# Soft mixture of experts inside a three-stage model: where the first weight transposes, the experts' loops and the combine weights' softmax stand

## Chip, cores and metric

The kernel runs on one core of a Trainium2 chip, in one launch. The metric is the time on the device in microseconds (us), the median of several runs. The inputs are drawn from a fixed seed, and all arithmetic is in float32.

## What is computed

Two blocks with a residual each, over x of shape (2, 1024, 256):

```python
x = x + L0_ffn(L0_cond(x, cond), phi, W, b)     # attention with 16 heads, then the soft mixture
x = x + L1_ffn(L1_cond(x, cond), ...)           # a rotation, then two layers of windowed attention
```

The change lies in the soft mixture, `L0_ffn`, with 64 experts of 32 slots each (2048 slots):

```python
logits   = einsum("bmd,dnp->bmnp", x, phi)
dispatch = softmax(logits, axis=0)                          # over the two batches
combine  = softmax(logits.reshape(b, m, n * p), axis=-1)    # over all 2048 slots
slots    = einsum("bmd,bmnp->bnpd", x, dispatch)
y        = einsum("bnpd,nde->bnpe", slots, W) + b[None, :, None, :]
out      = einsum("bnpd,bmnp->bmd", y, combine)
```

## The kernel before

The order of work on TensorE (PE), VectorE (DVE) and ScalarE (ACT) is written out by hand: inside a `manual_schedule` block each of these engines takes its instructions in the order in which the Python code issues them, and waits in that order. SyncE (SP) issues nearly all DMAs, also in one order. A tile pool hands out its buffers in turn, and a new tile waits until the last reader of the buffer's previous holder is done.

**First half of the mixture.** A loop over `it` from 0 to 31 takes a block of 512 slots (`n`) and a block of 128 tokens of each batch (`m`). `logits(it)` (L795) makes the logits of both batches in PSUM, copies them into a tile `keep` (ACT L803, DVE L806), issues two stores of 256 KB from `keep` to a scratch tensor `lgd` (L808), and takes the softmax over two batches as two sigmoids (L810, L811). `keep` has a ring of two buffers. `dispatch(it)` (L821) adds into the slots; at `m == 7` the sums are copied to the tile `slots`, batch 0 by ACT (L830) and batch 1 by DVE (L831). `experts(g0)` multiplies two groups of four experts by their weights (L842), 32 matmuls into one PSUM tile `py`, and adds the bias (DVE L851); it then issues the loads of the next two groups, 1 MB each (L778).

**Second half.** `ebig` holds four rows of 128 tokens by 2048 slots, row i in place i % 4. For each row, `fetch` (L864) brings the logits back from `lgd` in four pieces, `heaviest(i)` finds the maximum (DVE L868, L869), `weigh(i)` takes the exponential and its sum (ACT L875) and `scale(i)` divides (DVE L880, L881). `turn_w(q, jj)` transposes one of four pieces of rows 2q and 2q + 1 (PE L888, eight transposes into PSUM), copies it to a place in `xb` (ACT L895 for odd `jj`, DVE L897 for even `jj`), and issues the fetches of the same piece of rows 2q + 4 and 2q + 5. `combine(q, jj)` multiplies it by y (PE L909, eight matmuls); after `jj == 3` the result is added to x (DVE L920). The copies of `turn_w` cannot use `xb` before the last `dispatch`, since `xo_tm`, the tokens that `dispatch` reads, lies in the same memory.

PSUM tiles of `logits`, `turn_w`, `experts` and `rotate` all come from one ring of two buffers, `wide`. The loop around the change runs `q` from 0 to 3 and, within it, `jj` from 0 to 3: each round issues `turn_w` of the next piece, then `combine` of this one, then steps of the softmax of later rows; `rotate(0)` (L929, four matmuls of 512 columns) comes in round `q == 2`. Rounds 4 to 7 are interleaved with the next stage.

Of the kernel before, what the change touches and what calls it, by code (L numbers as in the profile page):

```python
# [10 lines left out]
F32 = mybir.dt.float32  # L11
# [6 lines left out]
P = 128  # L18
B = 2
S = 1024  # L20
# [71 lines left out]
def tile_kernel(ctx: ExitStack, tc: tile.TileContext, a: dict, out: bass.AP):  # L92
# [23 lines left out]
    xb = res.tile([P, 2, B, S + 1], F32, name="xb")  # L116
# [597 lines left out]
    for u in range(len(units)):  # L714
        if u % 2 == 0 and u + 2 < len(units):
            b, g = units[u + 2]
# [29 lines left out]
    with tc.manual_schedule(  # L746
        engines={mybir.EngineType.PE, mybir.EngineType.DVE, mybir.EngineType.Activation}
    ):
        for s in range(STEPS):
            u, p = s // 16, s % 16 // 2  # L750
# [38 lines left out]
    def logits(it):  # L789

        n, m = divmod(it, 8)
        lg = wide("lg")
        for b in (1, 0):
            for k in range(2):
                nc.tensor.matmul(  # L795
                    lg[:, b, :],
                    xa[:, k, b, 1 + m * P : 1 + (m + 1) * P],
                    phi[:, k, n * 512 : (n + 1) * 512],
                    start=(k == 0),
                    stop=(k == 1),  # L800
                )
        keep = dx0.tile([P, B, 512], F32, tag="keep", name="keep")
        nc.scalar.copy(keep[:, 1, :], lg[:, 1, :])  # L803
        l1 = dx0.tile([P, 512], F32, tag="l1", name="l1")
        nc.vector.tensor_tensor(l1, lg[:, 0, :], keep[:, 1, :], ALU.subtract)  # L805
        nc.vector.tensor_copy(keep[:, 0, :], lg[:, 0, :])  # L806
        for b in range(B):
            nc.sync.dma_start(lgd[b * 8 + m][:, n * 512 : (n + 1) * 512], keep[:, b, :])  # L808
        dsps[it] = dx0.tile([P, B, 512], F32, tag="dsp", name="dsp")
        nc.scalar.activation(dsps[it][:, 0, :], l1, AF.Sigmoid)  # L810
        nc.scalar.activation(dsps[it][:, 1, :], l1, AF.Sigmoid, scale=-1.0)  # L811

    def dispatch(it):

        n, m = divmod(it, 8)
        if m == 0:
            accs[n] = [pair(f"sl{b}") for b in range(B)]
        d = dsps.pop(it)
        for b in range(B):
            for c in range(2):  # L820
                nc.tensor.matmul(  # L821
                    accs[n][b][:, c, :],
                    xo_tm[:, b * 8 + m, c * P : (c + 1) * P],
                    d[:, b, :],
                    start=(m == 0),
                    stop=(m == 7),
                )
        if m == 7:
            slots[n] = dx.tile([P, 2, B, 512], F32, tag="slots", name="slots", bufs=1)
            nc.scalar.copy(slots[n][:, :, 0, :], accs[n][0])  # L830
            nc.vector.tensor_copy(slots[n][:, :, 1, :], accs[n][1])  # L831

    def experts(g0):

        py = wide("py").rearrange("p x (b d) -> p x b d", b=B)
        for x in range(2):
            w = ws.pop(g0 + x)
            for b in range(B):
                for k in range(2):
                    for n in range(4):  # L840
                        s0 = (4 * ((g0 + x) % 4) + n) * NP
                        nc.tensor.matmul(  # L842
                            py[n * NP : (n + 1) * NP, x, b, :],
                            slots[g0 // 4][:, k, b, s0 : s0 + NP],
                            w[:, n, k, :],
                            start=(k == 0),
                            stop=(k == 1),
                        )
        i = g0 % 4
        for b in range(B):  # L850
            nc.vector.tensor_tensor(y[b][:, g0 : g0 + 2, :], py[:, :, b, :], ybs[g0 // 4][:, i : i + 2, :], ALU.add)  # L851
        for g in (g0 + 2, g0 + 3):
            if g < NE // 4:
                weights(g)
# [11 lines left out]
    def heaviest(i):  # L866
        nmxs[i] = wsm.tile([P, 1], F32, tag="nmx", name="nmx")
        nc.vector.tensor_reduce(nmxs[i], row(i), AX.X, ALU.max)  # L868
        nc.vector.tensor_scalar(nmxs[i], nmxs[i], -1.0, None, ALU.mult)  # L869
# [8 lines left out]
    def scale(i):  # L878
        den = dens.pop(i)
        nc.vector.reciprocal(den, den)  # L880
        nc.vector.tensor_scalar(row(i), row(i), den, None, ALU.mult)  # L881

    def turn_w(q, jj):

        pt = wide("pe")
        for j in range(4):
            for i in range(2):
                nc.tensor.transpose(  # L888
                    pt[:, j // 2, (j % 2 * 2 + i) * P : (j % 2 * 2 + i + 1) * P],
                    row(2 * q + i)[:, (4 * jj + j) * P : (4 * jj + j + 1) * P],  # L890
                    ident,
                )
        wTs[q, jj] = xb[:, jj % 2, 1, 1 : 1 + S].rearrange("p (x n) -> p x n", x=2)
        if jj % 2:
            nc.scalar.copy(wTs[q, jj], pt)  # L895
        else:
            nc.vector.tensor_copy(wTs[q, jj], pt)  # L897
        for i in (2 * q + 4, 2 * q + 5):
            if i < T // P:
                fetch(i, jj)  # L900
# [68 lines left out]
    with tc.manual_schedule(  # L969
        engines={mybir.EngineType.PE, mybir.EngineType.DVE, mybir.EngineType.Activation}  # L970
    ):
        at_weigh = (1, 3, 4, 6)
        for g in range(2):
            weights(g)
        for it in range(3, ITS):
            n, m = divmod(it, 8)
            if it + 1 < ITS:
                logits(it + 1)
            dispatch(it)
            if n and m in (1, 4):  # L980
                experts(4 * n - 4 + m // 4 * 2)

            i = it - ITS + 8
            if 0 <= i < 4:
                for jj in range(4):
                    fetch(i, jj)
            if i - 1 in at_weigh:
                scale(at_weigh.index(i - 1))
            if i in at_weigh:
                heaviest(at_weigh.index(i))  # L990
                weigh(at_weigh.index(i))
        turn_w(0, 0)
        turn_w(0, 1)
        experts(12)
        combine(0, 0)
        turn_w(0, 2)
        combine(0, 1)
        turn_w(0, 3)
        combine(0, 2)
        experts(14)  # L1000
        dxs.close()
        for t in (xa, xb):
            nc.gpsimd.memset(t[:, :, :, 0:1], 0.0)


        load = {}
        wqo = pphi.tile([P, 4 * D * 4], F32, tag="phi", name="wqo")
        load["wqkv"] = wqo[:, : 6 * INNER].rearrange("p (k n) -> p k n", k=2)
        load["wo"] = wqo[:, 6 * INNER :].rearrange("p (k n) -> p k n", k=4)
        mask = dx0.tile([P, 4 * WIN], F32, tag="l1", name="mask")  # L1010
        nc.sync.dma_start(mask, a["mask"])

        def weights2(l, *names):
            for name in names:
                if name == "tabs":

                    load[name] = [dx0.tile([P, 2, 8, DH], F32, tag="dsp", name=f"tabs{l}{y}") for y in range(2)]
                    for y, t in enumerate(load[name]):
                        nc.sync.dma_start(t, a["tabs"].rearrange("p (x y) w d -> y p x w d", y=2)[y])
                        for x, of in enumerate((("qs", "ks"), ("qsr", "ksr"))[y]):  # L1020
                            nc.gpsimd.tensor_tensor(
                                t[:, x], t[:, x], bcast(rows[:, ROWS[f"{of}{l}"]], 1, 8), ALU.mult
                            )
                    continue
                k = {"wqkv": 2, "wo": 4, "w1": 2, "w2": NF}[name]
                whole = HID // P if name == "w2" else k
                nc.sync.dma_start(
                    load[name][:, :whole, :], a[name][l, : whole * P].rearrange("(c p) n -> p c n", p=P)
                )
                if whole < k:  # L1030
                    for r0 in (0, TG):
                        nc.sync.dma_start(load[name][r0 : r0 + TAIL, whole, :], a[name][l, whole * P :])

        weights2(0, "wqkv", "tabs", "wo")
    with tc.manual_schedule(
        engines={mybir.EngineType.PE, mybir.EngineType.DVE, mybir.EngineType.Activation}
    ):
        for q in range(4):
            for jj in range(4):
                if q == 0 and jj < 3:  # L1040
                    continue
                turn_w(*divmod(4 * q + jj + 1, 4))
                combine(q, jj)

                i = 2 * q + 2 + jj
                if q and 1 <= jj < 3:
                    scale(i - 1)
                if q and jj < 2:
                    heaviest(i)
                    weigh(i)  # L1050
                if q == 2 and jj == 1:
                    rotate(0)
# [619 lines left out]
```

## Time and profile before

Times are from one profiled execution, in us from its start.

| | |
|---|---|
| median of 3 runs | 1625.15 us (1624.53 to 1625.74) |
| the profiled execution | 1625.17 us, of which the span from first to last instruction is 1623.2 |
| granted TensorE clock | 0.999 |
| PE busy 750 to 800 / 800 to 885 us | 48.90 of 50 / 83.09 of 85 |
| DVE busy, the same | 23.59 / 48.13 |
| ACT busy, the same | 16.14 / 30.03 |
| DMA engines' busy share, the same | 0.71 / 0.33 |

A row of the timeline gives start, duration, engine, line, operation, output tile <- inputs, tile shape, and in brackets the idle time of that engine just before it with what ended it. One fp32 matmul appears as two records, a transpose as one. A row of the waits gives who waited, for whom, the total in us, how often, and the longest.

The first half of the mixture ends at 763 us and the rounds `q` 0 to 3 end at 848 us.

### The profile page before, as it was taken

How to read it: one execution, taken by the hardware profiler on the slowest of the kernel's cores; microseconds unless marked ns; L12 is line 12 of the kernel's file. 1: busy time of each engine (PE TensorE's matmuls, PEld its weight loads, DVE VectorE, ACT ScalarE, POOL GpSimd, SP SyncE). 2: the span in 40 equal slices, each digit the busy share in tenths (PEclk: the TensorE clock that was granted, in tenths of full speed). 3: DMA queues.
4: the chain of work that ended last, by engine and by line, in shares of the span. 5: the costliest groups of instructions: out<-in, count | busy, mean ns of one | idle time of the engine just before them, and what ended most of it. 6: DMA issues, size and time to landing. Idle time of an engine off the chain costs nothing.

```text
span 1623.2 us, 22628 instructions
## 1 busy us (share of the span) xinstructions
PE 1591.8 (98%) x8660; PEld 803.4 (49%) x8660; DVE 941.9 (58%) x1605; ACT 884.8 (55%) x1653; POOL 538.3 (33%) x830
## 2 busy tenths in 40 slices
PE   8999999999999999999999999999999999999998
PEld 4333333333333444444877676555555555655543
DVE  4768758776763122225446755757576666666632
ACT  2477767777886222235234544656657575656531
POOL 3233323333330100000103434555565555465411
PEclk9999999999999999999999999999999999999999
DMA  5100000010000544546532002000100001000001
GB/s 157 52 14 14 1 16 12 1 21 8 1 1 27 169 141 151 178 148 195 184 126 78 27 1 80 1 1 1 65 1 0 14 1 54 1 6 22 14 14 39
DMA packets 49707, 82.65 MB, mean 51 GB/s; under 512 B 4536, under 2 KB 24928, under 8 KB 49344
## 3 DMA queue, kind: packets, MB, share of 16 engines
q1 hardware_dynamic: 47056, 75.38, 15.0%
q0 software_dynamic: 1584, 5.29, 1.1%
q8 instruction: 68, 1.11, 0.3%
q10 hardware_dynamic: 960, 0.56, 0.1%
q14 instruction: 39, 0.32, 0.1%
HBM read 56.04 MB, written 20.97 MB: 47 GB/s over the span
## 4 chain that ended last, share of the span: by engine, by line
PE 89%; DVE 6%; ACT 2%; POOL 1%; issue 1%; DMA 1%; DVEq 0%; ACTq 0%; POOLq 0%
PE pga L1371 8%; PE sc L329 8%; PE po L347 7%; PE pm L295 7%; PE lg L795 7%; PE sl L821 7%; PE pq L1121 6%; PE cmb L909 5%; PE pwo L1310 3%; PE po L1290 3%; PE sc L1210 3%; PE py L1396 3%; PE pv L1177 3%; PE pe L1271 3%; PE pqk L265 2%; PE py L842 2%
## 5 line engine op out<-in xcount | busy, mean ns | idle before, releaser
L302 DVE TENSOR_REDUCE mx<-pm 128x2 f32<-128x1024 f32 x256 | 302.5, 1220 | 117.9 <-PE pm L295 117.3
L337 ACT ACTIVATE e<-sc 128x512 f32<-128x512 f32 (+1 forms) x500 | 266.2, 611 | 72.2 <-PE pm L295 44.6
L329 PE MATMUL sc<-qs,km 32*128 32x512 f32 x1024 | 254.7, 619 | 0.9 <-DVE qs L317 0.9
L295 PE MATMUL pm<-km,qm 32*128 32x512 f32 x1024 | 246.0, 619 | 2.4 <-ACT xa L432 0.6
L365 POOL TENSOR_TENSOR ob<-ob,part 128x512 f32<-128x512 f32 x101 | 128.4, 1271 | 270.2 <-ACT part L364 270.2
L1227 DVE CUSTOM_DVE_ANT_0 e<-sc,mask,zn 128x256 f32<-128x256 f32 (+1 forms) x256 | 102.3, 463 | 69.5 <-PE sc L1210 69.5
L1371 PE MATMUL pga<-hc,w 128*128 128x512 f32 x320 | 141.1, 593 | 0.0
L1260 POOL TENSOR_SCALAR e<-e,den 128x256 f32<-128x256 f32 (+1 forms) x128 | 131.1, 1038 | 27.0 <-DVE den L1256 27.0
L347 PE MATMUL po<-e,v 128*32 128x512 f32 x1024 | 136.7, 604 | 0.0
L329 PEld LDWEIGHTS sc<-qs,km 32*128 32x128 f32 x1024 | 87.5, 183 | 84.6 <-ACT e L337 64.4
L1244 ACT ACTIVATE e<-e,nmx 128x256 f32<-128x256 f32 (+1 forms) x256 | 123.5, 485 | 1.9 <-DVE nmx L1227 1.6
L1145 POOL TENSOR_TENSOR t<-raw,tabs 128x512 f32<-128x512 f32 x64 | 81.5, 1295 | 124.8 <-ACT raw L1135 119.6
L1121 PE MATMUL pq<-wqo,xa 128*128 128x512 f32 x256 | 115.9, 595 | 1.6 <-DVE xb L897 0.9
L909 PE MATMUL cmb<-xb,y 128*128 128x256 f32 x512 | 116.6, 380 | 0.2 <-ACT xb L895 0.2
L795 PE MATMUL lg<-phi,xa 128*128 128x512 f32 x256 | 115.9, 595 | 0.3 <-ACT xa L432 0.3
L821 PE MATMUL sl<-dsp,xb 128*128 128x512 f32 x256 | 114.9, 592 | 0.0
L295 PEld LDWEIGHTS pm<-km,qm 32*128 32x128 f32 x1024 | 82.8, 183 | 60.0 <-DVE mx L302 31.7
L805 DVE TENSOR_TENSOR l<-lg,keep 128x512 f32<-128x512 f32 x32 | 22.1, 692 | 143.5 <-ACT keep L803 143.5
L909 PEld LDWEIGHTS cmb<-xb,y 128*128 128x128 f32 x512 | 94.9, 190 | 16.6 <-issue 3.2
L1135 ACT COPY raw<-pq 128x1024 f32<-128x1024 f32 x32 | 32.4, 1013 | 128.6 <-PE pq L1121 126.8
L1371 PEld LDWEIGHTS pga<-hc,w 128*128 128x128 f32 x320 | 59.2, 190 | 67.2 <-issue 63.9
L803 ACT COPY keep<-lg 128x512 f32<-128x512 f32 x32 | 18.7, 585 | 125.1 <-issue 107.4
(212 smaller groups left out, 2491.2 us busy)
## 6 DMA issues: line engine op xcount, KB each, us to landing
lgd<-keep SPq DMA_DIRECT2D x64, 256.0 KB, 2.4
w<-in_ffn_W SPq DMA_DIRECT2D x16, 1024.0 KB, 7.5
ebig<-lgd SPq DMA_DIRECT2D x64, 256.0 KB, 3.3
wqo<-in_wqkv SPq DMA_DIRECT2D x2, 1536.0 KB, 8.6
w<-in_w SPq DMA_DIRECT2D x2, 1386.0 KB, 5.9
km<-hk SPq DMA_DIRECT2D x32, 64.0 KB, 2.3
qm<-hq SPq DMA_DIRECT2D x32, 64.0 KB, 2.3
phi<-in_phi SPq DMA_DIRECT2D x1, 2048.0 KB, 7.6
```

What stands on the lines that cost most here:

```text
L295: nc.tensor.matmul(pm[:, x, :], qm[u % 2][r, i * P : (i + 1) * P], km[u % 3][r, n * 512 : (n + 1) * 512], start=True, stop=True,)
L302: nc.vector.tensor_reduce(mxs[hu][:, i % 4, 2 * half : 2 * half + 2, n], pm, AX.X, ALU.max)
L329: nc.tensor.matmul(sc[:, x, :] if both else sc[x], km[u % 3][r, j * P : (j + 1) * P], qs[u % 2][r, n * 512 : (n + 1) * 512], start=True, s ...
L337: nc.scalar.activation(part, t, AF.Exp, scale=1.0 / HD0**0.5)
L347: nc.tensor.matmul(po[32 * hh : 32 * hh + 32, :], v[b][:, j, at : at + 32], es[s, hh // 2][:, hh % 2, :], start=True, stop=True,)
L365: nc.gpsimd.tensor_tensor(obs[u, n], obs[u, n], part, ALU.add)
L795: nc.tensor.matmul(lg[:, b, :], xa[:, k, b, 1 + m * P : 1 + (m + 1) * P], phi[:, k, n * 512 : (n + 1) * 512], start=(k == 0), stop=(k == 1),)
L821: nc.tensor.matmul(accs[n][b][:, c, :], xo_tm[:, b * 8 + m, c * P : (c + 1) * P], d[:, b, :], start=(m == 0), stop=(m == 7),)
L909: nc.tensor.matmul(acs[q][:, c, :], y[b][:, 4 * jj + j, c * P : (c + 1) * P], eT[:, j // 2, j % 2 * 256 : (j % 2 + 1) * 256], start=(jj == ...
L1121: nc.tensor.matmul(pq[:, x, :], shifted(xa, k, b, w * WIN, P), load["wqkv"][:, k, x * 512 : (x + 1) * 512], start=(k == 0), stop=(k == 1),)
L1260: engine.tensor_scalar(e[:, x, c, lo:], e[:, x, c, lo:], den[:, x, c : c + 1], None, ALU.mult)
L1371: nc.tensor.matmul(pt[:, x, :], load["w1"][:, k, lo : lo + P], hcs[f][:, k, :], start=(k == 0), stop=(k == 1))
```

## The change

It has three parts. `experts` goes batch by batch over both weight groups instead of group by group over both batches. `turn_w(0, 0)` is issued before the last `dispatch`, and its copy goes to a tile of its own, `wT`, in the ring of `keep`. In the rounds `q` 1 to 3 the maximum and the exponential of the first row of the next pair are issued at the end of the round before (`jj == 3`), those of the second row at `jj == 0`, and the two scalings at `jj == 0` and `jj == 1`; before, these steps stood at `jj` 0 and 1 and at `jj` 1 and 2.

```diff
@@ experts
-        for x in range(2):
-            w = ws.pop(g0 + x)
-            for b in range(B):
+        groups = [ws.pop(g0 + x) for x in range(2)]
+        for b in range(B):
+            for x, w in enumerate(groups):
                 for k in range(2):
                     for n in range(4):
@@ turn_w
-        wTs[q, jj] = xb[:, jj % 2, 1, 1 : 1 + S].rearrange("p (x n) -> p x n", x=2)
+        if (q, jj) == (0, 0):
+
+            wTs[q, jj] = dx0.tile([P, 2, 512], F32, tag="keep", name="wT")
+        else:
+            wTs[q, jj] = xb[:, jj % 2, 1, 1 : 1 + S].rearrange("p (x n) -> p x n", x=2)
@@ the loop over it
             if it + 1 < ITS:
                 logits(it + 1)
+            if it == ITS - 1:
+                turn_w(0, 0)
             dispatch(it)
@@
-        turn_w(0, 0)
         turn_w(0, 1)
         experts(12)
         combine(0, 0)
@@ the rounds
                 turn_w(*divmod(4 * q + jj + 1, 4))
                 combine(q, jj)

-                i = 2 * q + 2 + jj
-                if q and 1 <= jj < 3:
-                    scale(i - 1)
                 if q and jj < 2:
+                    scale(2 * q + 2 + jj)
+                if q and jj == 0 or q < 3 and jj == 3:
+                    i = 2 * q + 3 + (jj == 3)
                     heaviest(i)
                     weigh(i)
                 if q == 2 and jj == 1:
                     rotate(0)
```

## The prediction, made before the changed kernel ran

> **What bounds the kernel now.** I read the page first (busy times, then the chain that ended last), because they say whether a change that only reorders work can pay at all.
>
> ```profile
> PE 1591.8 (98%) x8660; PEld 803.4 (49%) x8660; DVE 941.9 (58%) x1605; ACT 884.8 (55%) x1653; POOL 538.3 (33%) x830
> PE 89%; DVE 6%; ACT 2%; POOL 1%; issue 1%; DMA 1%; DVEq 0%; ACTq 0%; POOLq 0%
> ```
>
> TensorE (PE) is busy 1591.8 of 1623.2 us. No matmul is removed here, so the change can only win back idle PE time, 31.4 us in all. Next I read the waits of PE alone, from 755 to 850 us, where every moved step lies. These two rows are all there is:
>
> ```profile
> PE pe L888 <- DVE ebig L881: 1.7, 2, 0.8
> PE py L842 <- ACT xb L895: 1.1, 1, 1.1
> ```
>
> Three stalls, then. The timeline gives what each costs from start to start, which is more than the idle shown, since PE refills after it.
>
> ```profile
> 763.37 1.91 PE L888 MATMUL pe<-ident,ebig 128*128 128x128 f32 x16
> 766.38 3.66 PE L842 MATMUL py<-w,slots 128*32 128x256 f32 x64 [1.10 <-ACT xb L895]
> ...
> 803.27 0.27 PE L888 MATMUL pe<-ident,ebig 128*128 128x128 f32 x1
> 804.38 0.98 PE L888 MATMUL pe<-ident,ebig 128*128 128x128 f32 x7 [0.84 <-DVE ebig L881]
> 805.20 3.62 PE L909 MATMUL cmb<-xb,y 128*128 128x256 f32 x16
> ```
>
> An undisturbed piece is eight transposes, 0.87 us (790.27 to 791.14), then a combine, 3.46 (795.48 to 798.93). The 16 transposes from 763.37 should take 1.75 and take 3.01: stall 1, before the experts, costs 1.26. Stall 2 costs 805.20 - 803.27 - 0.87 = 1.06; stall 3, from 842.43 to 844.36, the same. Were all three to vanish with nothing new in their place, 3.38 us would be won.
>
> **The change, part by part.** I read the order of each engine's instructions in both built programs, and place the durations of the trace on it.
>
> *Experts batch by batch.* The same 32 matmuls per call, 3.59 us (766.38 to 769.97). The second weight group is wanted after 8 of them instead of 16, 0.9 us sooner, and the first group's buffer comes free 0.9 us later, which moves one 1 MB load by as much in SP's queue. The cover: the last such load is issued at 770.10, lands 10.5 us later, at 780.6, and its experts start at 782.29, so some 2 us remain. Cost 0; if that cover were gone, up to the 0.9. The bias additions L851 (two in 1.29 us) are waited for by nobody on PE in the window, so having them sooner is worth 0.
>
> *First weights turned ahead of the last dispatch.* Eight transposes (0.87 us) now stand before the last four dispatch matmuls instead of behind them: nothing on PE itself. But the copy out of PSUM writes a new tile, wT, in a buffer of the ring "keep", and in the built program it waits for the previous holder's stores to land: those of the logits of step 30. VectorE (DVE) is in order, so the slots copy L831 and the scaling of row 3 sit behind that wait, and the experts' PSUM tile py takes the bank that this copy frees. So PE waits for the store, plus one copy. Of the store, two rows of SP's timeline and the landing row of the first of those three stores alone:
>
> ```profile
> 756.69 0.37 SPq L1027 DMA_DIRECT2D wqo<-in_wqkv  x1
> 757.15 2.34 SPq L808 DMA_DIRECT2D lgd<-keep  x3
> DMA to landing us min/median/max: 8.9/8.9/8.9
> ```
>
> The 39 stores from 600 to 757 us land in 2.3/2.4/5.9 (min/median/max). It goes out right behind a 1.5 MB weight load. Nothing ahead of it in SP's queue moves, so it lands at 757.15 + 8.88 = 766.04. The copy then takes 1.22 and its release 0.05 to 0.1 (row 766.10, and the stall rows): PE starts the experts at 767.35 instead of 766.38, +0.97. The slots copy ends at 768.4, before the second batch asks for it (767.35 + 1.8). The bounds of this unknown: a store that lands within 5.9 us holds nobody, and the experts start at 756.50 + 6.87 + 1.75 = 765.12, which is -1.26; one that lands as late as the tabs load in this stretch, 10.4 us, gives +2.5. I take +0.97, from the row of this very store. The two fetches that the moved turn_w issues pass the loads of mask and the first tabs in SP's queue, 512 KB ahead of them; POOL scales the tabs from 770.70 to 777.3 and then clears a column of xb, which the DVE copy at 787.23 waits for, so 10 us cover it: cost 0, and us for us beyond them.
>
> The Trainium skill speaks against that row: "DMA: Bandwidth & Descriptors", section on the anatomy of one DMA (software path), fits a transfer as 2.0 us plus its bytes at 436 GB/s, which for 256 KB makes an estimate of 2.6 us. By that rule the store has landed at 759.8, before the transposes end, and the whole sum below would be +0.6 us; the 8.9 us of the row decides, since the fit has no load queued ahead.
>
> *Maximum and exponential a step ahead.* In each of three rounds (q = 1, 2, 3) heaviest() and weigh() of the first row move one piece up. Of the first round, the rows of DVE, ACT and PE:
>
> ```profile
> 791.14 2.28 DVE L868 TENSOR_REDUCE nmx<-ebig 128x1 f32<-128x2048 f32 x1
> 793.45 0.15 DVE L869 TENSOR_SCALAR nmx<-nmx 128x1 f32<-128x1 f32 x1
> 791.39 1.01 ACT L895 COPY xb<-pe 128x1024 f32<-128x1024 f32 x1 [11.39 <-PE pe L888]
> 793.64 2.00 ACT L875 ACTIVATE ebig<-ebig,nmx 128x2048 f32<-128x2048 f32 x1 [1.23 <-DVE nmx L869]
> 802.71 0.99 ACT L895 COPY xb<-pe 128x1024 f32<-128x1024 f32 x1
> 795.48 3.62 PE L909 MATMUL cmb<-xb,y 128*128 128x256 f32 x16
> ```
>
> On DVE the maximum cannot start sooner: it already runs straight behind the additions L920. On ScalarE (ACT) two instructions change places: the exponential L875 now stands ahead of the copy L895 of piece jj = 1, ready since 791.31. The copy goes from 791.39 to 793.64 + 2.00 = 795.64 (a copy right behind an exponential starts 2.00 after it: 800.71, 802.71), ends at 796.65, and the combine L909 that reads it starts at 796.71 instead of 795.48: a new stall of 1.23, and about 0.09 of refill (the stalled combine at 884.48 takes 3.55 to the next start instead of 3.46). Three rounds have it, rows 791, 812 and 833: 3 x 1.32 = 3.96. What is won is stalls 2 and 3, 2.12; round q = 2 has no old stall, since rotate(0) covers it there with 3.43 us of matmuls. Net +1.84.
>
> The second exponential and the scaling are then early by enough: scale() of the second row ends near 803.3, and the transposes that read it come at 804.6. A last cover is thin. The DVE copy of piece jj = 2 now stands behind a scale and a maximum, ends at 799.55 + 1.23 = 800.78, and PE wants it at 801.1; if those 0.3 us are lost, each further us costs one, per round.
>
> After 850 us the orders of all engines are the same as before and move as a block. Sum: 0.97 + 1.84 = +2.8 us. The profiled execution took 1625.17 us (span 1623.2 and 2.0 around it), which is the median of the three runs, 1625.15, to 0.02. So 1628.0 us, +0.17%. A measurement of this kernel tells about 0.2%, here 3.25 us, from no change: the borders are 1621.9 and 1628.4.
>
> **The rivals.**
>
> *Slower: the store lands later still.* Place: the wait of the wT copy. Price: one us of PE per us, since copy, bank and experts follow in one chain. It decides from 0.45 us on, where the sum passes 3.25. For it: the DMA engines are busy for 0.71 of the time from 750 to 800 us (0.49 from 580 to 750), tabs took 10.4 us, and mask, a load of the same 256 KB issued 2.4 us after the store, took 9.9. Against it: what is queued ahead is unchanged, and mask and tabs now go out later. With 10.4 us: +2.5 + 1.84 = +4.3, 1629.5 us.
>
> *The copy is not held.* The store lands inside 5.9 us, or the copy's wait falls into time that PE has anyway: -1.26 + 1.84 = +0.6, 1625.8 us. For it, the 39 earlier stores; against it, the row.
>
> *All three stalls vanish*, the change doing what its name says: -1.26 - 2.12 = -3.4, 1621.8 us. It would need the ACT copy of jj = 1 to go ahead of the exponential; the built order has it behind.
>
> **How the numbers follow.** Forecast 0.66, with its own range of 1627.2 to 1628.8 (0.5 us on the landing, 0.1 on each stall, 0.6 of run-to-run spread); about a fifth of it lies over 1628.4. Later store 0.24, counted as slower; copy not held 0.07, counted as the same; all stalls gone 0.03, counted as faster. Slower by over 0.2%: 0.24 + 0.14 = 0.38; faster: 0.03; the same: 0.59. The range leaves out the two low cases and the far end of the later store: 1626.5 to 1629.7.
>
> **What would show it.** Right: PE's waits name L842 behind the DVE copy of wT with about 2.1 us idle, and three waits of the combine behind the ACT copy near 796, 815 and 838, about 1.2 each; the waits behind L881 are gone from this stretch; busy PE unchanged. Wrong: wT copied before 763 us, a combine that does not wait, or a wait behind the DVE copy of jj = 2.

## The result, and the profile after

The changed kernel takes 1628.88 us (median of 11 runs, 1627.78 to 1630.77) against 1625.19 for the kernel before (11 runs): ratio 1.0023, 95% interval 1.0013 to 1.0032, or +3.7 us. The forecast was +2.8. The execution that was profiled is the longest of the eleven: 1630.77 us, span 1628.9. Two executions far off all others, one of the kernel before (2318.75 us) and one of the first version of kernel 6 (8263.87 us), are left out of the ratios below.

First the page of the changed kernel: its busy times, and its chain of work that ended last. (Lines above L890 keep their numbers; below, the copies are L899 and L901, the combine L913, the additions L924.)

```profile
PE 1593.7 (98%) x8660; PEld 805.0 (49%) x8660; DVE 940.8 (58%) x1605; ACT 884.6 (54%) x1653; POOL 538.2 (33%) x830
PE 90%; DVE 5%; ACT 2%; POOL 1%; issue 1%; DMA 1%; DVEq 0%; ACTq 0%; POOLq 0%
```

TensorE still bounds. But the same 8660 records are busy 1.9 us longer, which no term of the forecast allowed for. The waits of PE from 755 to 855 us:

```profile
PE cmb L913 <- ACT xb L899: 3.1, 3, 1.0
PE py L842 <- issue: 3.0, 1, 3.0
```

The three stalls of before are gone. Four new ones stand in their place: one before the experts and one in each of the rounds `q` 1 to 3. The chain behind the first, from the timeline (PE and DVE rows), then SP's rows, and the landing of the store issued at 756.98 alone, which is the second store of step 30:

```profile
764.06 1.04 PE L888 MATMUL pe<-ident,ebig 128*128 128x128 f32 x8
766.79 1.22 DVE L901 COPY wT<-pe 128x1024 f32<-128x1024 f32 x1 [5.94 <-DMA lgd<-keep]
768.12 5.35 PE L842 MATMUL py<-w,slots 128*32 128x256 f32 x64 [3.02 <-issue]
```

```profile
756.51 0.37 SPq L1032 DMA_DIRECT2D wqo<-in_wqkv  x1
756.98 2.34 SPq L808 DMA_DIRECT2D lgd<-keep  x3
```

```profile
DMA to landing us min/median/max: 9.7/9.7/9.7
```

DVE is idle for 5.94 us until the store of `keep` has landed, 756.98 + 9.7 = 766.7. The copy ends at 768.01, and the experts start 0.11 later. The waits put PE's idle down to "issue", but the two rows agree with a wait for the copy, and kernel 4 below shows it. The experts then take 5.28 us from their start to the start of the next matmuls (773.40), instead of 3.59. The stretches of the trace, cut where the clock's own records change, say why (columns: stretch, its length; busy time and instructions of PE, PEld, DVE, ACT, POOL; granted clock; DMA share, GB/s):

```profile
765.88:769.30 3.42, 1.18 (x24) 0.91 (x28) 2.47 (x4) 0.27 (x1) 0.00 (x0) 1.00 1.02 305
769.30:772.71 3.41, 3.41 (x40) 2.17 (x36) 1.24 (x1) 0.00 (x0) 0.76 (x1) 0.50 0.94 344
```

For 3.41 us after the idle PE ran at half its clock; such a stretch is called a spell from here on. It costs 5.28 - 3.59 = 1.69 us, which is most of the added 1.9 us of busy time.

The first of the three new stalls in the rounds, ACT's rows and PE's:

```profile
797.06 2.00 ACT L875 ACTIVATE ebig<-ebig,nmx 128x2048 f32<-128x2048 f32 x1 [13.63 <-DVE nmx L869]
799.06 0.99 ACT L899 COPY xb<-pe 128x1024 f32<-128x1024 f32 x1
800.10 2.21 PE L913 MATMUL cmb<-xb,y 128*128 128x256 f32 x9 [1.04 <-ACT xb L899]
```

The copy runs right behind the exponential, and the combine right behind the copy, as the order of the instructions said.

### The profile page after: what moved, and what is told of

Same layout as the page of the kernel before. It is cut to its first block, busy times and chain, and to the rows that moved or that the text cites. A ratio compares the mean times of both kernels' runs of the same rounds, so it can differ in the third digit from the quotient of the medians.

```text
span 1628.9 us, 22626 instructions
## 1 busy us (share of the span) xinstructions
PE 1593.7 (98%) x8660; PEld 805.0 (49%) x8660; DVE 940.8 (58%) x1605; ACT 884.6 (54%) x1653; POOL 538.2 (33%) x830
## 4 chain that ended last, share of the span: by engine, by line
PE 90%; DVE 5%; ACT 2%; POOL 1%; issue 1%; DMA 1%; DVEq 0%; ACTq 0%; POOLq 0%
PE pga L1376 8%; PE sc L329 8%; PE po L347 7%; PE pm L295 7%; PE lg L795 7%; PE sl L821 7%; PE cmb L913 6%; PE pq L1126 6%; PE pwo L1315 3%; PE po L1295 3%; PE sc L1215 3%; PE py L1401 3%; PE pv L1182 3%; PE pe L1276 3%; PE pqk L265 2%; PE py L842 2%
## 5 line engine op out<-in xcount | busy, mean ns | idle before, releaser
L913 PE MATMUL cmb<-xb,y 128*128 128x256 f32 x496 | 113.2, 381 | 3.4 <-ACT xb L899 3.4
L795 PE MATMUL lg<-phi,xa 128*128 128x512 f32 x256 | 115.9, 595 | 0.3 <-ACT xa L432 0.3
L913 PEld LDWEIGHTS cmb<-xb,y 128*128 128x128 f32 x496 | 92.0, 190 | 19.6 <-ACT xb L899 4.5
```

The lines of the kernel that those rows point to most:

```text
L795: nc.tensor.matmul(lg[:, b, :], xa[:, k, b, 1 + m * P : 1 + (m + 1) * P], phi[:, k, n * 512 : (n + 1) * 512], start=(k == 0), stop=(k == 1),)
L913: nc.tensor.matmul(acs[q][:, c, :], y[b][:, 4 * jj + j, c * P : (c + 1) * P], eT[:, j // 2, j % 2 * 256 : (j % 2 + 1) * 256], start=(jj == ...
```

## The experiments

Theory H: the copy of `wT` is held by the store, and the ACT copy by the exponential; the long idle of PE can bring a spell of half clock. The rivals are named in the expectations: R and C (another part of the change carries the loss), B and S (another cause of the wait), D and E (of the cures). Every kernel with a ratio was timed beside the kernel before. The table also gives PE's times from start to start in the profiled execution, in us: from the dispatch of step 30 to the experts behind it, these experts themselves, and the rounds from `experts(14)` on, up to the next stage's first matmul (tile `pq`). They do not depend on the rest of an execution, as the total does.

| kernel | ratio to before, 95% | dispatch(30) to experts(12) | experts(12) | experts(14) to first `pq` |
|---|---|---|---|---|
| before | | 9.88 | 3.59 | 65.52 |
| changed | 1.0023 (1.0013 to 1.0032) | 11.80 | 5.28 | 67.33 |
| changed, once more | 1.0025 (1.0015 to 1.0034) | 11.81 | 3.59 | 67.34 |
| 1: loops alone | 0.9999 (0.9990 to 1.0008) | 9.88 | 3.59 | 65.52 |
| 2: transposes alone | 1.0015 (1.0006 to 1.0024) | 11.41 | 5.50 | 65.52 |
| 3: rounds alone | 1.0008 (0.9999 to 1.0017) | 9.88 | 3.59 | 67.33 |
| 4: changed, wT's own buffer | 1.0000 (0.9992 to 1.0009) | 8.71 | 3.59 | 67.33 |
| 5: changed, loads on POOL's queue | 1.0003 (0.9994 to 1.0012) | 8.71 | 3.59 | 67.34 |
| 6: changed, three filler matmuls | 1.0015 (1.0006 to 1.0024) | 11.29 | 3.59 | 67.33 |
| 7: changed, ACT copy first | 1.0015 (1.0006 to 1.0024) | 11.59 | 3.59 | 65.64 |
| 8: before, maximum ahead | 0.9983 (0.9975 to 0.9992) | 9.88 | 3.59 | 63.41 |
| 9: maximum ahead and 4 | 0.9976 (0.9967 to 0.9985) | 8.71 | 3.59 | 63.41 |

**1 to 3, one part each on the kernel before.** The edits are the three parts of the diff, each by itself.

> The first part alone, on the kernel before: the experts batch by batch. Theory H: 0 us; every call of the experts takes 3.59 us from start to next start, and the loads of the next weights stay covered. Rival C (the order of the loops makes the experts slow, or uncovers a weight load): +0.9 to +1.7 us, a call that takes over 4 us or waits for its weights.

> The second part alone, on the kernel before: the first transposes ahead of the last dispatch, their copy in the ring of keep. Theory H (held copy): the copy of wT waits for the store behind the 1.5 MB load, the experts start 11 to 12 us after the dispatch of step 30 instead of 9.88; with the spell of half clock that the changed kernel shows at 769 us, PE loses 1 to 2 us by the wait and up to 1.7 us by the clock: about +1.9 us over the kernel before (the measured +3.7 less the +1.84 of the rounds), range +1.0 to +3.6. Rival R (the rounds carry everything): 0 to +0.5 us, experts start as before.

> The third part alone, on the kernel before: maximum and exponential a step ahead. Theory H: three combines wait behind the ACT copy, 1.04 us of idle each, the waits behind L881 are gone: +1.84 us, 1.5 to 2.2. Rival R: the rounds carry all of the measured +3.7 us.

Medians 1625.55, 1626.98 and 1626.66, against 1625.34, 1625.57 and 1625.57 of the kernel before, timed beside them. The loops cost nothing: rival C is out. The rounds lose 67.33 - 65.52 = 1.81 us, which is half of the loss and not all of it: rival R is out. Its ratio alone, with an interval that reaches to no difference, would not show it; the row of the table does. The transposes carry the rest, and the profile of that kernel has the spell too:

```profile
764.68:768.09 3.41, 1.36 (x24) 0.70 (x28) 2.66 (x4) 0.46 (x1) 0.00 (x0) 1.00 1.02 307
768.09:771.50 3.41, 3.41 (x40) 1.69 (x36) 1.05 (x1) 0.00 (x0) 0.40 (x1) 0.50 0.96 347
```

The three medians add up to +2.7 us and not to +3.7. Each is known to about 1.5 us only, so it is the rows of the table that divide the loss.

**4, a buffer that no store holds.** On the changed kernel:

```diff
-            wTs[q, jj] = dx0.tile([P, 2, 512], F32, tag="keep", name="wT")
+            wTs[q, jj] = dx.tile([P, 2, 512], F32, tag="wT", bufs=1, name="wT")
```

> The changed kernel with wT in a buffer of its own, so that its copy waits for no store. Theory H: the copy runs at about 761 us, the experts start some 8.8 us after the dispatch of step 30 (9.88 before, 11.80 in the changed kernel), no idle of 3 us, so no spell of half clock there and the experts take 3.59 us again: -1.26 + 1.84 = +0.6 us over the kernel before, -3.1 against the changed one. Rival C (the slow experts come from the new loop order, not from the wait): start as in H, but the experts still take 5.3 us: +2.3. Rival B (the experts wait for something else, such as the bank or the slots): no change, +3.7.

The order of all instructions is the same as in the changed kernel; only the copy's waits for two stores are gone. DVE's and PE's rows:

```profile
759.81 1.23 DVE L901 COPY wT<-pe 128x1024 f32<-128x1024 f32 x1
763.04 1.04 PE L888 MATMUL pe<-ident,ebig 128*128 128x128 f32 x8
764.01 3.66 PE L842 MATMUL py<-w,slots 128*32 128x256 f32 x64
```

The experts start 8.71 us after the dispatch, 3.1 sooner than in the changed kernel, and take 3.59. Rivals B and C are out. Against before the two stretches give -1.17 + 1.81 = +0.6; the median was 1624.97 against 1625.57, which the interval cannot tell from that or from nothing.

**5, the two loads of `wqo` on another queue.** On the changed kernel:

```diff
-                nc.sync.dma_start(
+                (nc.gpsimd if l == 0 and name in ("wqkv", "wo") else nc.sync).dma_start(
```

> The changed kernel with the loads of wqkv (1.5 MB) and wo (0.5 MB) issued on POOL's queue instead of SP's, so that the store of the logits does not stand behind them in its queue; the DMA engines are shared as before. Theory Q (the queue's order makes the store late): the store lands in 2.4 to 4 us, the copy of wT runs at about 760 us, the experts start 8.7 us after the dispatch of step 30: -3 us against the changed kernel, +0.6 over the kernel before. Rival S (the engines are shared, whatever the queue): the store still takes 8 us or more, the experts start 11 us or more after the dispatch: no gain.

The time is what theory Q gave: experts at 8.71, median 1625.49 against 1625.34. Its reason, the place in the queue, holds only in part. SP's rows, POOL's row of the load, and the landing of the store issued at 758.43:

```profile
755.00 2.43 SPq L808 DMA_DIRECT2D lgd<-keep  x2
757.48 0.43 SPq L1016 DMA_DIRECT2D mask<-in_mask  x1
758.43 0.32 SPq L808 DMA_DIRECT2D lgd<-keep  x1
```

```profile
756.72 0.73 POOL L1032 DMA_DIRECT2D wqo<-in_wqkv  x1 [69.47 <-PE lg L795]
```

```profile
DMA to landing us min/median/max: 9.9/9.9/9.9
```

The load has to wait for the last logits (POOL's row names L795), which read the memory it fills. On SP's queue it held the store of step 30 behind it until 0.66 us after the dispatch's start. With the load on POOL's queue that store goes out at 755.00, 1.25 us before the dispatch (756.25) and 1.7 us before the load, and the copy of `wT` runs at 760.76 without a wait. The view gives no landing for this store; the records of its semaphore in the trace end at 757.40, which makes 2.4 us. The same records give 4.0 us for the store at 757.11, 0.4 us behind the load (its last record stands at 761.09). The store at 758.43 takes 9.9 us, though in its own queue only another store and `mask` (256 KB each) were issued since the load. So a store behind the load can be as slow with the load on another queue, as rival S says, but need not be. What helped `wT` is that its store went out before the load.

**6, PE kept busy in the idle.** First six matmuls of 512 columns between `turn_w(0, 1)` and `experts(12)`, then three:

```diff
         turn_w(0, 1)
+        fill = pair("fill")
+        for j in range(3):
+            nc.tensor.matmul(fill[:, 0, :], ident, xo_tm[:, 0:2, :], start=True, stop=True)
         experts(12)
```

> The changed kernel with six matmuls of 512 columns, whose result nobody reads, in the idle before the experts: 6 x 0.43 = 2.6 of the 3.0 us. The wait for the copy stays. Theory H with the clock: the experts start at the same time, 11.8 us after the dispatch of step 30, but the clock is not halved and they take 3.59 instead of 5.28 us: -1.7 us against the changed kernel, +2.0 over the kernel before. Rival C (loop order): the experts still take 5.3 us, no gain, +3.7.

> The filler again with three matmuls of 512 columns instead of six, since one such fp32 matmul is two records of 0.43 us: 3 x 0.86 = 2.6 us, inside the 3.0 us of idle. Theory H with the clock: experts start 11.4 to 11.8 us after the dispatch of step 30, no halved clock there in the profile, experts 3.59 us. The median falls by the share of executions that had the spell times 1.7: -0.8 to -1.7 us against the changed kernel, so +2.0 to +2.9 over the kernel before. Rival C: the experts stay at 5.3 us, no gain.

With six: median 1630.78 us (1629.86 to 1631.15 in the six executions that count), ratio 1.0032 (1.0020 to 1.0043). The size was wrong: 0.43 us is one record, and an fp32 matmul has two. So the six took some 5.2 us, an estimate from the row below (six records in 2.7 us), and ran past the end of the wait. With three, PE's rows:

```profile
764.14 2.74 PE L1001 MATMUL fill<-xb,ident 128*128 128x512 f32 x6
766.81 3.66 PE L842 MATMUL py<-w,slots 128*32 128x256 f32 x64
```

The start stays late and the experts take 3.59. The median, 1628.13, lies 0.8 us under the changed kernel's, at the near end of what H gave and inside the spread. By itself this does not show that the filler kept the clock up: the next run has no spell either, without a filler.

**The changed kernel once more.**

> The changed kernel itself once more, for another execution in the profiler. Theory H with the clock: experts start 11.3 to 11.8 us after the dispatch of step 30, an idle of 2.6 to 3 us before them and, where the 3.413 us windows of the clock fall as in the first profile, a spell at half clock right behind it and experts of 5.3 us; median +3 to +4 us over the kernel before.

1629.06 against 1625.13 us. The same wait, 3.03 us of idle, and no spell this time. The same cuts of the trace:

```profile
763.07:766.49 3.42, 1.89 (x11) 1.12 (x9) 0.00 (x0) 1.68 (x2) 0.00 (x0) 1.00 1.08 235
766.49:769.90 3.41, 1.91 (x36) 1.44 (x40) 3.20 (x4) 0.00 (x0) 0.00 (x0) 1.00 1.05 357
769.90:773.32 3.42, 3.42 (x43) 2.50 (x33) 1.80 (x3) 0.00 (x0) 1.52 (x2) 1.00 0.95 322
```

The clock's changes lie on a grid of 3.413 us (in the first profile the spell begins 757.76 us, 222 such steps, after the first record of full clock). Here an edge of that grid falls in the middle of the idle, so each of the two stretches keeps 1.9 us of PE work. In the first profile one stretch had 1.18. This pair of profiles also gives the loss without a spell: span 1626.6 against 1623.2, made of 1.93 before the experts, 1.82 in the rounds, and -0.3 before the stretch; what lies behind it differs by less than 0.1.

**7, the two ACT instructions exchanged.** On the changed kernel, `weigh` of the first row after `turn_w(q, 1)` again, `heaviest` where the change put it:

```diff
                 combine(q, jj)
+                if q and jj == 0:
+                    weigh(2 * q + 2)
                 if q and jj < 2:
                     scale(2 * q + 2 + jj)
-                if q and jj == 0 or q < 3 and jj == 3:
-                    i = 2 * q + 3 + (jj == 3)
-                    heaviest(i)
-                    weigh(i)
+                if q < 3 and jj == 3:
+                    heaviest(2 * q + 4)
+                if q and jj == 0:
+                    heaviest(2 * q + 3)
+                    weigh(2 * q + 3)
```

> The changed kernel with the ACT copy of piece jj = 1 put ahead of the exponential again; maximum and second row stay where the change put them. Theory H (the thin cover): the combine of piece 1 no longer waits, but the DVE copy of piece 2, which stands behind the second maximum, ends at the same time as before the edit and is now wanted 1.2 us sooner: three waits of the combine behind the DVE copy, about 0.9 us of idle each, take the place of the three behind ACT. -0.5 to -0.7 us against the changed kernel. Rival E (the exchange of the two ACT instructions is all that is wrong with the rounds): no waits in the rounds, -4.0 us against the changed kernel.

PE's waits, and the rows of DVE and PE for one of them:

```profile
PE cmb L913 <- DVE xb L901: 1.7, 2, 0.9
```

```profile
801.00 1.22 DVE L901 COPY xb<-pe 128x1024 f32<-128x1024 f32 x1
802.27 3.73 PE L913 MATMUL cmb<-xb,y 128*128 128x256 f32 x16 [0.85 <-DVE xb L901]
```

The new wait came as H has it, behind the DVE copy, 0.85 us each; rival E is out (1626.99 us, not 1624.9). But there are two such waits, not three: in round `q == 2` `rotate(0)` covers the copy, which the expectation had missed. The rounds gain 1.69 us against the changed kernel where 0.5 to 0.7 was expected, and stand at 65.64, 0.12 above the kernel before.

**8 and 9, the maximum ahead of the additions.** `heaviest(2q + 4)` is issued at `jj == 3` between `turn_w` and `combine`, so that it runs while PE multiplies; `weigh` follows. In kernel 8 this stands on the kernel before, in kernel 9 on the changed kernel together with the edit of 4. The lines taken out below are those of the changed kernel; the lines that come out are the same in both:

```diff
                 turn_w(*divmod(4 * q + jj + 1, 4))
+                if q < 3 and jj == 3:
+                    heaviest(2 * q + 4)
                 combine(q, jj)
+                if q < 3 and jj == 3:
+                    weigh(2 * q + 4)
                 if q and jj < 2:
                     scale(2 * q + 2 + jj)
-                if q and jj == 0 or q < 3 and jj == 3:
-                    i = 2 * q + 3 + (jj == 3)
-                    heaviest(i)
-                    weigh(i)
+                if q and jj == 0:
+                    heaviest(2 * q + 3)
+                    weigh(2 * q + 3)
```

> The kernel before with one edit: the first maximum of the next pair ahead of the additions of the result, the rest of the softmax of the rounds as in the best version. Theory H: stalls 2 and 3 vanish, stall 1 of 1.26 stays: -2.1 us against the kernel before, and +1.3 against the best version. Rival D (the best version owes its time to the experts' part): 0.

> A version that should beat both kernels: wT in its own buffer, and in the rounds the first maximum is issued ahead of the additions of the result (it then runs while PE multiplies), so that the exponential comes 2 us earlier and the ACT copy behind it is in time. Theory H: all three stalls of the kernel before vanish and none takes their place: -3.4 us against the kernel before (-1.26 - 2.12), no waits of PE from 755 to 850 us; rounds of 59.8 us instead of 61.9 (start of the second transposes' block to the first pq). Rival D (the maximum ahead of the additions finds its fetch not landed, or the copy of piece 2 becomes late): the rounds stay at 61 us or more, -1 us in all.

8: 1622.37 against 1625.13 us; -2.1 lies inside its interval, so rival D of this run is out. The 1.3 us that it should be behind kernel 9 do not show in the medians (0.3 apart, timed at different times); the table's first column shows 1.17. 9: 1622.07 against 1625.34, faster than both kernels. Of kernel 9, the DVE and ACT rows of the first round, and the two stretches from 750 to 850 us:

```profile
785.98 2.28 DVE L868 TENSOR_REDUCE nmx<-ebig 128x1 f32<-128x2048 f32 x1
788.36 0.74 DVE L924 TENSOR_TENSOR xT<-xT,cmb 128x256 f32<-128x256 f32 x2
788.48 2.00 ACT L875 ACTIVATE ebig<-ebig,nmx 128x2048 f32<-128x2048 f32 x1 [10.86 <-DVE nmx L869]
790.48 0.99 ACT L899 COPY xb<-pe 128x1024 f32<-128x1024 f32 x1
```

```profile
750.00:800.00 50.00, 50.00 (x329) 36.32 (x328) 24.48 (x30) 19.13 (x21) 5.05 (x5) 1.00 0.72 224
800.00:850.00 50.00, 50.00 (x253) 41.38 (x252) 25.20 (x29) 15.20 (x15) 1.90 (x2) 1.00 0.39 121
```

The maximum ends at 788.26, 0.2 us after the combine that the additions wait for (784.43 + 3.62), and nothing on PE waits for the additions' later start. The exponential starts 4.05 us after the start of that combine, against 6.83 in the kernel before (786.81, 793.64), and the ACT copy is done at 791.5, before the combine that reads it (793.10). PE has no idle left in 100 us. The rounds gain 2.11 us (2.12 was expected), the experts' part 1.17 (1.26).

## Why the prediction was right or wrong

*The time:* 1628.88 us lies inside the range, and 0.08 us past the forecast's own narrower one. At +0.23% it is past the border of 0.2%, a side to which the chances gave 0.38 against 0.59 for no difference. The range reached that far because of the rival of a later store, and that rival came in part.

*What bounds the kernel, and the loops:* right. The loops cost 0 in kernel 1, and the cover of the weight loads held: each of the eight `experts` took 3.59 us there.

*The copy of `wT`:* the chain was right, store, copy, bank, experts, and its size was not. The term was +0.97 us; it measured +1.92 and +1.93 in the two profiles of the changed kernel, +1.4 to +1.7 in kernels 2, 6 and 7. The mis-sized step is the landing, taken as 8.88 from one row; it measured 9.7. In the four profiles with the old order the same store took 8.5 to 9.2 us; in the seven where the transposes are moved and the load stays on SP's queue, 9.2 to 9.7. Besides, the copy starts 0.11 us after the landing, which the sum left out. Why the store is later in the new order was not tried; its place behind the load is unchanged. What the new order sends out sooner, while the store is under way, are the two fetches of the moved transposes (760.71 instead of 764.32); that they delay it is not shown. The rival of the later store, which was to decide from 0.45 us on, is nearly this: the store landed 0.8 us later than reckoned, past that point, and not at the 10.4 that the rival was priced with. The wait came under the name "issue", and 3.0 us long where 2.1 was told.

*The clock:* absent from the forecast, which said that busy PE would be unchanged. The wait was reckoned at its own length; that a wait of 3 us can slow the work behind it was not weighed, though the profile of the kernel before, with a granted clock of 0.999, has a spell of its own at 1039.6 us. Where the spell comes it costs 1.7 (changed) to 1.9 us (kernel 2), and it came in two of the four profiles that have an idle of 2.6 us or more there. How often it comes in unprofiled executions is not settled, so the measured +3.7 cannot be split to the tenth: the waits alone make 1.93 + 1.82 = 3.75, and with the copy as held in kernel 2, 3.3.

*The rounds:* right. 1.81 us in kernel 3 against 1.84, three waits of 1.04 shown. From start to start each costs 1.21, and the combine behind it takes 0.10 longer: 3 x 1.31 - 2.12 = 1.81.

*The thin cover of 0.3 us at the DVE copy of piece 2:* it held in the changed kernel. Kernel 7 shows that it was as thin as told: once the combine before it came sooner, that copy was late.

*The rules weighed:* the Trainium skill, "DMA: Bandwidth & Descriptors", anatomy of one DMA, gave an estimate of 2.6 us for this store. In kernel 5 the same store, issued ahead of the load, took 2.4 us by its semaphore's records, near that estimate. Behind the load it took 8.5 to 9.7 us in the eleven other profiles of the table, and the row, not the rule, had to be used.

## What to carry to other kernels

A tile that is put into a ring also takes over the ring's waits: ask what the previous holder is still doing, and price its store where it stands among the loads, with the spread of several executions and not one row. Before an exponential is pulled ahead on an in-order engine, ask which copy it passes and who reads that copy; here the gain lay in starting the chain of maximum, exponential and scaling sooner, in DVE time that was idle, and not in exchanging two instructions. A long wait of TensorE can cost more than its length: here 3.0 us of idle brought 1.69 us of half clock on top in one profile, and nothing in another.

## What the runs showed of the hardware

The granted clock fell to 0.50 for one step of its 3.413 us grid after a step in which PE was busy for 1.18 us (changed kernel) or 1.36 us (kernel 2), and stayed at 1.00 after steps with 1.82, 1.89, 1.91 and 2.20 us (kernel 7 and the changed kernel once more). Transposes counted as work: without their 1.04 us the step of 1.89 us would hold only 0.85, and it kept the clock. Another idle place, near 1040 us, brings none, one or two steps of half clock in the profiles of these kernels. There the clock fell after steps with 0.98 to 1.69 us of PE work and stayed after steps with 1.63 to 2.25. So the border lies at about 1.6 to 1.8 us of the 3.413, about half, and PE's busy time as the profile counts it does not place it more closely. Much of the spread goes with the clock: timed beside kernel 7, the kernel before ran 1622.3 to 1622.6 us where the granted clock was 1.000, and 1625.4 to 1627.3 where it was 0.997.

The Trainium skill, "TensorE: Matmul & The Clock Gate", Part 1, "What's actually happening", has a free-running window of 3413 ns, which these records show, and gives as the condition for the half clock at least one idle window of about 3.4 us. Here 3.0 us of idle, and in kernel 2 2.6 us, were enough when they fell mostly into one window; the measurement decides.
